# Counting put-off rows four tiles at a time in a graph-network kernel, with their scatters pinned in GpSimd's order

## The chip, the cores and the metric

The kernel runs on one core of a Trainium2 chip. The metric is the device time of one execution in microseconds (us). A NeuronCore has a matrix engine (TensorE, PE in the profile, with its weight loads as PEld), a vector engine (VectorE, DVE), a scalar engine (ScalarE, ACT), GpSimd (POOL) and SyncE (SP), which only issues transfers. Each engine runs its own instructions in their order and waits on semaphores for the others.

## The reference

Four graph layers run one after the other over 4096 nodes with 256 features and one 4096 x 4096 adjacency matrix `adj`; after each, `x = layernorm(x + layer(x))`. Layers 0, 2 and 3 multiply the adjacency with the features and apply a weight matrix. Layer 1 takes two steps of attention in which each row keeps only its largest probabilities, up to a mass of 0.9:

```python
def _top_p_attention(X, W1, W2, W3):
    logits = (X @ W1.T @ W2.T) @ (X @ W3.T).T
    probs = softmax(logits, axis=-1)
    idx = argsort(-probs, axis=-1)
    cs = cumsum(sorted probs)
    mask = cs - sorted probs < 0.9          # put back in the row's order
    A = probs * mask
    return A / max(A.sum(-1, keepdims=True), 1e-12)

R = S + eye; R = R / R.sum(-1, keepdims=True)        # here S is adj
for n in range(2):
    A = _top_p_attention(Xa, W1, W2, W3)
    Xf = R @ Xf
    Xa = A @ Xa
    Z = Z + Xf @ U1[n].T + Xa @ U2[n].T
return layernorm(X + Z) * ln_g + ln_b
```

## The kernel before

The 4096 rows are 32 tiles of 128 rows (`NT = 32`, `P = 128`). The program runs in this order: layer 0, attention step 0, attention step 1, layers 2 and 3 (whose matmuls are L175).

Each attention step is a loop in `run_step` over iterations i = -2 to 31, software-pipelined over three tiles. In iteration i the logits of tile i + 2 are made in eight chunks (L414 on PE, copied by ACT at L415); for tile i + 1, the candidate called `cd`, DVE finds the cut (`peak_groups` with MAX8 at L433, the maximum at L465 and L466, then `tops` with L528 and L532, `pick` to L564); tile i is multiplied (`pieces`). In step 0 a row keeps few entries, so the product of tile i gathers 16 rows of x per row through GpSimd (`gather`, L672) and multiplies by diagonals (L761). In step 1 the row of probabilities is masked by DVE (`settle`: a match-replace over 4096 columns at L658, then the mask in four quarters at L663), transposed by PE (`turn`, L744), copied by ACT (L747) and multiplied (L767). Beside it run the products of R (`neighbours`, L683, L686, ended by L688), one row tile in most iterations, and for the finished tile `mix` (L820, L822) and, in step 1, two layer norms (the power on GpSimd at L199, then L846 and L204). `settle` of tile i + 1 must be done before `pieces` of tile i + 1 begin.

`ops` is a dictionary: `at(g, f)` runs f after piece g (0 to 7) of the iteration. A scheduler then reorders instructions on each engine by its own estimates, within what data and buffers allow, but not across a conditional block (`tc.If`).

**Put-off rows.** Some rows cannot be cut by the quick search. `pick` sets `bad` to 1 for them. `flag` (L582) counts them: PE multiplies `bad` with a matrix of ones (L592, the tile's number of bad rows in every partition) and with a strictly triangular matrix (L593, the bad rows ahead of each one); DVE adds the running base (L595), forms a slot for each row (L599, L600), and GpSimd scatters the row numbers into a list in DRAM (L606). Rows that are not bad go to spare slots. PE, DVE and POOL thus each take part once per tile, in piece 4 of the iteration.

Later the listed rows are worked off in groups of 128 (`put_off`): read the list (L886, L888), gather the rows, make a query and logits, the peak (L471), five probes for the threshold (L498), candidates (L512, L433), tops, pick, a conditional exact search (L648), and `settle` with three match-replaces and the mask. It is a generator: `advance(job)` runs it to its next `yield`, at pieces 1 and 6 of each iteration. `LATER = (1, 3)` gives one group in step 0 and three in step 1; `starts` says after which iteration each begins, and `finish` runs what is left of one before the next and multiplies its rows:

```python
starts = {min((k + 1) * NT // LATER[n] - 1, NT - 2): k for k in range(LATER[n])}
```

That is iteration 30 in step 0, and 9, 20 and 30 in step 1. The groups of step 1 are called the first, second and third here. After iteration 31 the second group's product runs beside 16 tiles of the next layer's `zu` (L869), and the third group's work beside the other 16; then a rest loop (`left_over`) runs zero or more times. `half("mm")` gives the two halves of one PSUM bank (`mm_bank`) in turn, for counting, queries and `mix`.

Of the kernel before, what the change touches and what calls it, by code (L numbers as in the profile page):

```python
# [40 lines left out]
LATER = (1, 3)  # L41
ROUNDS = 9
NG_LATER = 18
KEPT = 16
MATCHES_LATER = 3
MATCHES = 1
# [10 lines left out]
def gnn_stack(ctx, tc, x, adjt, adjn, w0, b0, w1, w2t, w3t, u1t, u2t, ln_g, ln_b, w2, b2, w3, b3, out):  # L57
# [28 lines left out]
    def half(bank):  # L86
        turns[bank] ^= 1
        return (mm_bank if bank == "mm" else acc_bank)[:, turns[bank], :]
# [268 lines left out]
    with tc.tile_pool(name="l1", bufs=1, reuse_waits="tile") as l1:  # L357
# [64 lines left out]
        def small(tag, w=1, dt=F32, bufs=2):  # L422
            if cur["late"]:
                return cur["lw"].tile([P, w], dt, tag=tag, name=f"{tag}_l", bufs=2 if w == 1 else 1)
            return work.tile([P, w], dt, tag=tag, name=tag, bufs=bufs)
# [108 lines left out]
        def pick(st, rounds):  # L534

            top, thr, base = st["top"], st["thr"], st["base"]
            W = 8 * rounds  # L540
            cs = small("cs", W + 1, bufs=1)
            if base is None:
                nc.vector.memset(cs[:, 0:1], 0.0)
                te = small("te", W + 1)
                nc.scalar.activation(te, top, AF.Exp, bias=st["m"], scale=1.0)
            else:
                nc.vector.tensor_copy(cs[:, 0:1], base)
                te = top
            nc.vector.memset(cs[:, W:], 3e38)
            nc.vector.tensor_tensor_scan(cs[:, 1:W], te[:, : W - 1], te[:, : W - 1], cs[:, 0:1], op0=ALU.add, op1=ALU.max)  # L550
            under, part = small("under", W, bufs=1), small("part", W, bufs=1)
            count = small("count")
            nc.vector.tensor_scalar(under, cs[:, :W], thr, 0.0, op0=ALU.is_lt, op1=ALU.add, accum_out=count)
            nc.vector.scalar_tensor_tensor(part, cs[:, 1:], thr, under, op0=ALU.is_ge, op1=ALU.mult)
            st["t"] = t = small("t_thr")
            nc.vector.scalar_tensor_tensor(part, part, 1.0, te[:, :W], op0=ALU.mult, op1=ALU.mult, accum_out=t)
            st["left"] = left = small("left")
            nc.vector.tensor_scalar(part, te[:, :W], t, 0.0, op0=ALU.is_ge, op1=ALU.add, accum_out=left)
            nc.vector.tensor_sub(left, left, count)
            st["bad"] = bad = small("bad")  # L560
            nc.vector.tensor_tensor(bad, te[:, W - 1 : W], te[:, W:], op=ALU.max)
            nc.vector.tensor_tensor(bad, bad, t, op=ALU.is_ge)
            most = 0.0 if sparse(st) else 8.0 * (MATCHES if base is None else MATCHES_LATER)
            nc.vector.scalar_tensor_tensor(bad, left, most, bad, op0=ALU.is_gt, op1=ALU.max)  # L564
            if sparse(st):

                same = small("same")
                for r in range(8, W, 8):
                    nc.vector.tensor_tensor(same, top[:, r - 1 : r], top[:, r : r + 1], op=ALU.is_equal)
                    nc.vector.tensor_tensor(bad, bad, same, op=ALU.max)  # L570
                st["w"] = w = small("w", W)
                kept = small("kept")
                nc.vector.scalar_tensor_tensor(w, te[:, :W], t, te[:, :W], op0=ALU.is_ge, op1=ALU.mult, accum_out=kept)
                whole(st, kept)
# [7 lines left out]
        def flag(st):  # L582


            pb = half("mm")
            later = st.get("later")
            if later is None:
                nc.tensor.matmul(pb[:1, 0:1], st["bad"], ones_col, start=True, stop=True)
                st["nb"] = small("nbad", 1, I32)[:1, :]
                nc.scalar.copy(st["nb"], pb[:1, :1])  # L590
                return
            nc.tensor.matmul(pb[:, 0:1], ones_sq, st["bad"], start=True, stop=True)  # L592
            nc.tensor.matmul(pb[:, 1:2], before, st["bad"], start=True, stop=True)  # L593
            sofar, slot = small("sofar"), small("slot")
            nc.vector.tensor_add(sofar, later["base"], pb[:, 0:1])  # L595

            i = st["tile"]
            at, rows_i = slots_of[cur["n"]][:, i : i + 1], ids[:, i : i + 1]
            nc.vector.scalar_tensor_tensor(slot, pb[:, 1:2], later["base"], spare, op0=ALU.add, op1=ALU.subtract)  # L599
            nc.vector.scalar_tensor_tensor(at, slot, st["bad"], spare, op0=ALU.mult, op1=ALU.add)  # L600
            later["base"] = sofar
            if i == NT - 1 and cur["n"] == 0:

                st["to"] = to = small("to_last", 1, I32, 1)
                nc.vector.scalar_tensor_tensor(to, st["bad"], float(P), rows_i, op0=ALU.mult, op1=ALU.add)
            nc.gpsimd.indirect_dma_start(  # L606
                out=list_d[cur["n"]], out_offset=bass.IndirectOffsetOnAxis(ap=at, axis=0), in_=rows_i, in_offset=None)

        def bit_by_bit(st):

# [331 lines left out]
        def run_step(n, es):  # L942

            later = {"base": spare0}
            tiles = {}
            last = []
            jobs = []
# [26 lines left out]
                cur["late"] = False  # L976
                return [[f] for f in after(n, job["st"])]

            starts = {min((k + 1) * NT // LATER[n] - 1, NT - 2): k for k in range(LATER[n])}
            for i in range(-2, NT):  # L980
                st = tiles.pop(i, None)
                cd = tiles.get(i + 1)
                nxt = None
                if i + 2 < NT:

                    nxt = {"tile": i + 2, "q": cur["qs"].pop(0), "e": logits_in(es[i % 2]), "later": later, "G": {}}
                    tiles[i + 2] = nxt
                if i + 1 == NT and n == 0:
                    for fs in last:
                        for f in fs:  # L990
                            f()
                    last = []
                    left_over(n, es[NT % 2], later)
                ops = {}

                def at(g, f, *args):
                    ops.setdefault(g, []).append(lambda: f(*args))

                for g, fs in zip((1, 2), last):
                    for f in fs:  # L1000
                        at(g, f)
                if 0 < i + 2 < NT - 1:
                    turned = []
                    g = 1 if n else 6
                    at(g - 1, lambda i, turned: turned.append(transposed(cur["xa"][:, i + 3, :])), i, turned)
                    at(g, lambda turned: cur["qs"].append(query(None, turned[0])), turned)
                if cd is not None:
                    peak_groups(cd, NG_LATER if n else ngr)
                    at(1, exp_rows, cd)
                for job in jobs:  # L1010
                    at(1, advance, job)
                if cd is not None:
                    rounds = ROUNDS if n else KEPT // 8
                    at(2, tops, cd, rounds)
                    at(2, pick, cd, rounds)
                    at(4, flag, cd)
                    if n == 0:
                        for k in range(8):
                            at(4 + k // 2, gather, cd, k)
                    else:  # L1020
                        at(5, lambda cd: [None for _ in settle(cd)], cd)
                if n == 0 and st is not None:
                    for k in range(8, KEPT):
                        at(k // 2 - 4, gather, st, k)
                for job in jobs:
                    if n and i + 1 == NT:
                        at(4, advance, job)
                    at(6, advance, job)
                if i + 1 == NT and n == 0:
                    cur["next"] = load_halves(es[1 - NT % 2], xf_d, nc.sync)  # L1030
                if i < 0:
                    now = FIRST[n][i + 2]
                else:
                    now = [i + 2] if FIRST[n][1][-1] < i + 2 < NT else []
                pieces(n, st, nxt, ops, now)
                last = [[f] for f in after(n, st)] if st is not None else []
                if i in starts:
                    k = starts[i]
                    if len(jobs) > (i == NT - 2):
                        last = finish(jobs.pop(0), last)  # L1040
                    e = es[NT % 2] if k + 1 == LATER[n] else es[2]
                    jobs.append({"stages": put_off(n, k, e, later)})
                    if i < NT - 2:
                        advance(jobs[-1])
# [185 lines left out]
```

## Time and profile before

| what | us |
|---|---|
| median of 3 runs | 3214.06 (3208.3 to 3225.59) |
| the profiled execution's own time | 3106.69 |
| its span, from the first to the last instruction | 3105.0 |
| PE busy in it | 2902.2 (93%) |
| DVE busy | 2253.7 (73%) |
| ACT busy | 1725.0 (56%) |
| POOL busy | 779.8 (25%) |
| mean granted PE clock | 0.976 |

The profiled execution is 3.3% shorter than the median of the timed runs. Step 0 lies between about 360 and 1280 us of the span, step 1 from there to about 2550, layers 2 and 3 to the end. A line of the group view reads: source line, engine, operation, output and inputs by the program's names, shape, count, then times. An entry of the waits reads: who waited, for whom, total us, times, longest us. A line of the timeline reads: start, duration, engine, source line, operation, names, shape, number of merged instructions, and in brackets the idle time before it and what ended it. A row of the stretches reads: from and to, length, then busy time and number of instructions of PE, PEld, DVE, ACT and POOL, then the PE clock, the DMA share and GB/s.

### The profile page before, as it was taken

What the parts mean: (1) busy time and instruction counts of PE and PEld (TensorE: products, weight loads), DVE (VectorE), ACT (ScalarE), POOL (GpSimd) and SP (SyncE); (2) the same over time, 40 slices, a digit from 0 to 9 for tenths busy, and PEclk for the clock granted to TensorE, in tenths of its full rate; (3) what the DMA queues carried; (4) which work ended last, traced back from release to release, by engine and by line L of the source; (5) the groups of instructions that cost most, each with busy time, mean ns of one, the idle gap of its engine ahead of it and who ended that gap; (6) DMA issues with size and microseconds to landing.
All of it is one profiled execution on the core that took longest, in us unless ns stands there. A gap on an engine that the chain in (4) does not pass through costs nothing. (4 is left out here: it accounts for less than half of the span.)

```text
span 3105.0 us, 45412 instructions
## 1 busy us (share of the span) xinstructions
PE 2902.2 (93%) x14244; PEld 2300.0 (74%) x14244; DVE 2253.7 (73%) x7159; ACT 1725.0 (56%) x2883; POOL 779.8 (25%) x908
## 2 busy tenths in 40 slices
PE   7999889999999997799999999999999978999998
PEld 3788677788878875577777877878878546777886
DVE  4666688888888884379997999959998725443444
ACT  2555566666666655364555555546554426666664
POOL 1111167777777772000000000010001110000000
PEclk9999999999999998899999999999999998999999
DMA  9996378888878873310000111101111324333332
GB/s 170 158 176 136 66 131 138 164 153 154 147 153 155 161 149 112 117 50 25 25 21 25 37 34 38 30 31 35 39 35 32 115 88 152 107 107 97 107 107 78
DMA packets 247484, 299.44 MB, mean 96 GB/s; under 512 B 34464, under 2 KB 201312, under 8 KB 247232
## 3 DMA queue, kind: packets, MB, share of 16 engines
q0 software_dynamic: 46336, 104.28, 23.8%
q1 hardware_dynamic: 188656, 180.93, 18.9%
q10 hardware_dynamic: 12240, 11.23, 1.1%
q8 instruction: 115, 1.88, 0.3%
q14 instruction: 137, 1.12, 0.2%
HBM read 330.65 MB, written 66.32 MB: 128 GB/s over the span
## 5 line engine op out<-in xcount | busy, mean ns | idle before, releaser
L686 PE MATMUL acc_r<-xh,adjq 128*128 128x512 f32 x2048 | 617.1, 430 | 20.9 <-ACT adjq L683 12.0
L767 PE MATMUL acc_bank<-xa,at 128*128 128x256 f32 x2240 | 548.1, 385 | 25.8 <-ACT at L747 25.4
L672 POOL DMA_INDIRECT G<-x_d,cols x512 | 496.6, 970 | 214.4 <-PE acc_bank L761 77.6
L683 ACT CAST adjq<-adj 128x512 fp32r<-128x512 fp8e4 x512 | 316.2, 620 | 399.5 <-PE acc_r L686 318.8
L767 PEld LDWEIGHTS acc_bank<-xa,at 128*128 128x128 f32 x2240 | 408.4, 192 | 84.3 <-ACT at L747 37.1
L686 PEld LDWEIGHTS acc_r<-xh,adjq 128*128 128x128 f32 x2048 | 378.9, 191 | 110.4 <-ACT adjq L683 31.8
L433 DVE MAX8 cand<-e 128x8 f32<-128x228 f32 (+1 forms) x1088 | 386.6, 399 | 71.1 <-ACT e L415 69.5
L199 POOL TENSOR_TENSOR rstd<-ve,mhalf 128x1 f32<-128x1 f32 x166 | 100.3, 604 | 1330.9 <-DVE ve L197 1287.5
L415 ACT COPY e<-lg 128x512 f32<-128x512 f32 x544 | 315.0, 585 | 183.7 <-PE lg L414 179.9
L414 PE MATMUL lg<-kS,q 128*128 128x512 f32 x1088 | 385.0, 439 | 0.1
L1110 ACT CAST a<-a 128x1024 fp32r<-128x1024 fp8e4 x256 | 268.1, 1049 | 167.9 <-PE acc L175 127.9
L761 PE MATMUL acc_bank<-G,dg 128*128 128x256 f32 x1024 | 272.2, 387 | 12.5 <-DMA adj<-adj_d 5.4
L530 DVE FIND_INDEX8 cols<-top,e 128x8 uint32<-128x4096 f32 x64 | 282.8, 4419 | 0.0
L175 PE MATMUL acc<-xh,a 128*128 128x512 f32 x1024 | 261.9, 410 | 21.0 <-DMA x2i<-x_d 17.1
L175 PE MATMUL acc<-y0h,a 128*128 128x512 f32 x1024 | 250.0, 398 | 0.0
L175 PEld LDWEIGHTS acc<-xh,a 128*128 128x128 f32 x1024 | 193.5, 192 | 67.7 <-ACT xh L151 22.2
L175 PE MATMUL acc<-yh,a 128*128 128x512 f32 x1024 | 237.9, 394 | 0.0
L761 PEld LDWEIGHTS acc_bank<-G,dg 128*128 128x128 f32 x1024 | 196.6, 193 | 49.5 <-DVE dg L759 10.0
L175 PEld LDWEIGHTS acc<-yh,a 128*128 128x128 f32 x1024 | 192.3, 188 | 43.6
L175 PEld LDWEIGHTS acc<-y0h,a 128*128 128x128 f32 x1024 | 188.1, 188 | 38.8 <-issue 0.6
L747 ACT COPY at<-at_ps 128x512 f32<-128x512 f32 x288 | 168.8, 588 | 83.0 <-PE at_ps L744 81.3
L414 PEld LDWEIGHTS lg<-kS,q 128*128 128x128 f32 x1088 | 180.1, 192 | 20.4 <-ACT e L415 6.4
(287 smaller groups left out, 4430.3 us busy)
## 6 DMA issues: line engine op xcount, KB each, us to landing
adj<-adj_d SPq DMA_DIRECT2D x256, 128.0 KB
a<-adj_d SPq DMA_DIRECT2D x256, 128.0 KB
a<-in_adjt POOLq DMA_DIRECT2D x64, 256.0 KB
adj_d<-a SPq DMA_DIRECT2D x64, 256.0 KB
adjn<-in_adjn POOLq DMA_DIRECT2D x64, 256.0 KB
x_d<-x SPq DMA_DIRECT2D x64, 128.0 KB
xf_d<-xf_new SPq DMA_DIRECT2D x64, 128.0 KB
xf<-xf_d SPq DMA_DIRECT2D x64, 128.0 KB
```

The lines of the kernel that those rows point to most:

```text
L175: nc.tensor.matmul(acc, a[:, j, :], halves(jt), start=(jt == 0), stop=(jt == NT - 1))
L414: nc.tensor.matmul(pl[:, :LC], q[k], kS[:, s], start=(k == 0), stop=(k == 1))
L415: nc.scalar.copy(l[:, s], pl[:, :LC])
L433: nc.vector.max(dst[:, 8 * g : 8 * g + 8], src[:, g * w : min((g + 1) * w, N)])
L530: nc.vector.max_index(st["at"][:, 8 * r : 8 * r + 8], t8, st["e"][:, :N])
L672: nc.gpsimd.indirect_dma_start(out=g, out_offset=None, in_=x1_d, in_offset=bass.IndirectOffsetOnAxis(ap=st["at"][:, k : k + 1], axis=0))
L683: nc.scalar.copy(a, cur["a8"][:, g % 2 * GP : (g % 2 + 1) * GP, :])
L686: nc.tensor.matmul(acc_r, a[:, j, :], xf[:, jt, :], start=(jt == 0), stop=False)
L747: nc.scalar.copy(at[:, :G, :], ps[:, :G, :])
L761: nc.tensor.matmul(acc_a, dg[:, k % 4, :], st["G"][k], start=(k == 0), stop=(k == KEPT - 1))
L767: nc.tensor.matmul(acc_a, ats[g][:, j, :], cur["xa"][:, jt, :], start=(jt == 0), stop=(jt == NT - 1))
L1110: nc.scalar.copy(a, a8)
```

## The change

`flag` no longer counts each tile. `pick` writes `bad` into a column of a four-column tile `bads`; when the fourth column is full (tiles 3, 7, 11, ...), or for each of the last four tiles alone, one pair of matmuls counts all columns, a scan adds the running base, and four more DVE operations form the slots. The scatters are put on a list `pend` and issued singly: one from each `flag`, and one more at a fixed place in each iteration (piece 0 in step 0, piece 3 in step 1), and all that are left ahead of a group's start. Each is pinned behind the instructions traced before it on GpSimd. In step 1 `flag` moves from piece 4 to piece 7, and the counting matmul is pinned behind what PE was given before it. `starts` is rounded up to the next iteration i with i % 4 == 3: iterations 11, 23 and 30 in step 1 instead of 9, 20 and 30; in step 0 it stays 30.

```diff
+AT_ONCE = 4
...
-            st["bad"] = bad = small("bad")
+            later = st.get("later")
+            if later is None:
+                st["bad"] = bad = small("bad")
+            else:
+                if later["from"] is None:
+                    later["from"] = st["tile"]
+                    later["bads"] = work.tile([P, AT_ONCE], F32, tag="bads", name="bads", bufs=2)
+                c = st["tile"] - later["from"]
+                st["bad"] = bad = later["bads"][:, c : c + 1]
...
-            nc.tensor.matmul(pb[:, 0:1], ones_sq, st["bad"], start=True, stop=True)
-            nc.tensor.matmul(pb[:, 1:2], before, st["bad"], start=True, stop=True)
-            sofar, slot = small("sofar"), small("slot")
-            nc.vector.tensor_add(sofar, later["base"], pb[:, 0:1])
-
-            i = st["tile"]
-            at, rows_i = slots_of[cur["n"]][:, i : i + 1], ids[:, i : i + 1]
-            nc.vector.scalar_tensor_tensor(slot, pb[:, 1:2], later["base"], spare, op0=ALU.add, op1=ALU.subtract)
-            nc.vector.scalar_tensor_tensor(at, slot, st["bad"], spare, op0=ALU.mult, op1=ALU.add)
-            later["base"] = sofar
...
-            nc.gpsimd.indirect_dma_start(
-                out=list_d[cur["n"]], out_offset=bass.IndirectOffsetOnAxis(ap=at, axis=0), in_=rows_i, in_offset=None)
+            if i % AT_ONCE == AT_ONCE - 1 or i >= NT - AT_ONCE:
+                first, bads = later["from"], later["bads"]
+                w = i + 1 - first
+                later["from"] = None
+                pb = half("mm")
+                total = nc.tensor.matmul(pb[:, :w], ones_sq, bads[:, :w], start=True, stop=True)
+                if n:
+                    tc.keep_in_program_order(total)
+                nc.tensor.matmul(pb[:, AT_ONCE : AT_ONCE + w], before, bads[:, :w], start=True, stop=True)
+                sofar, slot = small("sofar", AT_ONCE + 1), small("slot", AT_ONCE)
+                nc.vector.tensor_copy(sofar[:, 0:1], later["base"])
+                nc.vector.tensor_tensor_scan(sofar[:, 1 : w + 1], pb[:, :w], bads[:, :w], sofar[:, 0:1], op0=ALU.add,
+                                             op1=ALU.max)
+                nc.vector.scalar_tensor_tensor(slot[:, :w], pb[:, AT_ONCE : AT_ONCE + w], spare, sofar[:, :w],
+                                               op0=ALU.subtract, op1=ALU.add)
+                nc.vector.tensor_mul(slot[:, :w], slot[:, :w], bads[:, :w])
+                nc.vector.tensor_scalar(slots_of[n][:, first : i + 1], slot[:, :w], spare, None, op0=ALU.add)
+                later["base"] = sofar[:, w : w + 1]
+                later["pend"] += range(first, i + 1)
+            scatter(later)
+
+        def scatter(later, most=1):
+
+            for k in later["pend"][:most]:
+                tc.keep_in_program_order(nc.gpsimd.indirect_dma_start(
+                    out=list_d[cur["n"]], out_offset=bass.IndirectOffsetOnAxis(ap=slots_of[cur["n"]][:, k : k + 1], axis=0),
+                    in_=ids[:, k : k + 1], in_offset=None))
+            later["pend"] = later["pend"][most:]
...
-            starts = {min((k + 1) * NT // LATER[n] - 1, NT - 2): k for k in range(LATER[n])}
+            starts = {}
+            for k in range(LATER[n]):
+                i = (k + 1) * NT // LATER[n] - 1
+                starts[min(i + (AT_ONCE - 1 - i) % AT_ONCE, NT - 2)] = k
...
+                if i < NT - 2:
+                    at(3 if n else 0, scatter, later)
...
-                    at(4, flag, cd)
+                    at(NLC - 1 if n else 4, flag, cd)
...
                 if i in starts:
+                    scatter(later, NT)
```

More of the change, by code (lines that the diff above doesn't have):

```diff
@@ L582, in flag @@
         def flag(st):
-            pb = half("mm")
             later = st.get("later")
             if later is None:
+                pb = half("mm")
                 nc.tensor.matmul(pb[:1, 0:1], st["bad"], ones_col, start=True, stop=True)
@@ L600, in flag @@
-            nc.vector.scalar_tensor_tensor(at, slot, st["bad"], spare, op0=ALU.mult, op1=ALU.add)
-            later["base"] = sofar
-            if i == NT - 1 and cur["n"] == 0:
-                st["to"] = to = small("to_last", 1, I32, 1)
-                nc.vector.scalar_tensor_tensor(to, st["bad"], float(P), rows_i, op0=ALU.mult, op1=ALU.add)
-            nc.gpsimd.indirect_dma_start(
-                out=list_d[cur["n"]], out_offset=bass.IndirectOffsetOnAxis(ap=at, axis=0), in_=rows_i, in_offset=None)
+            i, n = st["tile"], cur["n"]
@@ new lines, in flag @@
+            if i == NT - 1 and n == 0:
+                st["to"] = to = small("to_last", 1, I32, 1)
+                nc.vector.scalar_tensor_tensor(to, st["bad"], float(P), ids[:, i : i + 1], op0=ALU.mult, op1=ALU.add)
+            if i % AT_ONCE == AT_ONCE - 1 or i >= NT - AT_ONCE:
+                first, bads = later["from"], later["bads"]
+                w = i + 1 - first
+                later["from"] = None
+                pb = half("mm")
+                total = nc.tensor.matmul(pb[:, :w], ones_sq, bads[:, :w], start=True, stop=True)
[12 more added lines that the diff above has]
+                later["pend"] += range(first, i + 1)
@@ L942, in run_step @@
         def run_step(n, es):
-            later = {"base": spare0}
+            later = {"base": spare0, "from": None, "bads": None, "pend": []}
             tiles = {}
```

## The prediction, made before the changed kernel had run

> **What bounds the kernel now.** I read the tenths by slice first, then busy time by stretch, then the idle time before the counting matmuls (L592), then the order of time around them. The slices show TensorE (PE) full nearly throughout, and VectorE (DVE) full beside it only in the second attention step (slices 18 to 30):
>
> ```profile
> PE   7999889999999997799999999999999978999998
> DVE  4666688888888884379997999959998725443444
> ```
>
> Busy time in three stretches (us; PE, weight loads, DVE, ACT, POOL): the steady part of step 0, step 1 with the R products up to the maximum of tile 25, and from there to the first masked quarter of tile 31:
>
> ```profile
> 500.00:1150.00 650.00, 649.58 (x3685) 519.91 (x3684) 569.74 (x1692) 421.49 (x822) 477.61 (x506) 1.00 0.84 153
> ...
> 1656.00:2171.00 515.00, 490.07 (x2470) 405.95 (x2470) 450.78 (x1518) 285.35 (x480) 38.82 (x49) 0.98 0.12 33
> 2171.00:2393.00 222.00, 210.93 (x1073) 175.01 (x1073) 210.94 (x730) 117.79 (x194) 15.63 (x20) 1.00 0.15 32
> ```
>
> Step 0 is PE alone, without gaps, 24.43 us a tile. In the second stretch PE leads (490 of 515; gaps 26.5, of which 9.2 before L592), DVE has 59 us of gaps. In the third both stand at 95%: DVE is as full as PE.
>
> What one tile's counting costs PE in step 0, by the timeline (start, us):
>
> ```profile
> 720.31 0.40 PE L696 MATMUL nef_ps<-adjn,adj 128*128 128x128 fp8e4 x4
> 720.54 0.34 PE L592 MATMUL mm_bank<-bad,ones_sq 128*128 128x1 f32 x2
> 720.74 0.36 PE L593 MATMUL mm_bank<-bad,before 128*128 128x1 f32 x2
> 720.96 0.71 PE L414 MATMUL lg<-kS,q 128*128 128x512 f32 x2
> ```
>
> From 720.54 to 720.96, so 0.42 us, nothing else enters PE. In step 1 PE also waits there, because `bad` is not ready (us in total, times, longest; 1640 to 2400):
>
> ```profile
> PE mm_bank L592 <- DVE bad L564: 15.8, 15, 1.7
> ```
>
> Last, the end of step 1 on DVE: tile 31's maximum, its match-replace, its mask, its slots, and the list read back:
>
> ```profile
> 2375.41 0.30 DVE L465 TENSOR_REDUCE m<-cand 128x1 f32<-128x144 f32 x1
> ...
> 2386.81 4.43 DVE L658 MATCH_REPLACE8 e<-match,e 128x4120 f32<-128x4120 f32 x1
> 2391.41 1.28 DVE L663 SCALAR_TENSOR_TENSOR e<-e,t_thr 128x1024 f32<-128x1024 f32 x1
> 2393.46 0.21 DVE L600 SCALAR_TENSOR_TENSOR slots<-slot,bad,spare 128x1 int32<-128x1 f32 x1
> ...
> 2403.88 0.15 DVE L888 TENSOR_SCALAR from_l<-to_l 128x1 int32<-128x1 int32 x1 [6.01 <-DMA to_l<-list_d]
> ```
>
> PE cannot begin tile 31's transposes before L663, and the last put-off group cannot begin before the list. From there PE runs full to the end of the step (zu tiles, 84.6 us busy in 2420 to 2511), so what delays this point delays the end.
>
> **What the Trainium skill says.** "TensorE: Matmul & The Clock Gate", The mechanism: matmuls keep strict program order, so one that waits holds those behind it; the 15.8 us before L592 agree. "VectorE: DVE Perf Modes", Rules for kernel authors: minimize the number of operations, since each pays its own fixed part; agreed, as L595, L599 and L600 take 155, 211 and 204 ns for one column. "Perfetto Trace Analysis", Optimization Strategy: where a kernel has several regimes, interleaving them can help. The trace agrees that it does here: the second put-off group ends (L658 and L663 between 2275 and 2302) beside R products, and PE idled only 3.2 us between 2270 and 2320.
>
> **The change, part by part.**
>
> *Fewer countings, step 0.* 32 pairs become 11 (seven groups of four, then the last four tiles singly): 21 × 0.42 = 8.8 us less on PE, which is the bound. A pair of four columns isn't in the trace; it adds three columns to each matmul, and 1024 columns of L414 took 0.54 us (720.96 to 721.50), so under 0.01 us. **−8.8.** DVE's three operations give way to five a group; hidden, as DVE is at 88% here. GpSimd (POOL) issues the same 32 scatters, but two in some iterations and none in others. Its gathers (L672) start 1.25 us apart (711.75, 713.00), so 16 of them, two adjn loads and one scatter fill about 23.5 of the 24.4 us. A second scatter (1.16 us, L606) puts it about 1 us behind, and the next tile without one gives that back, with 12 gather buffers between: 0, at most +4 over the step if gathers come late.
>
> *First nine tiles of step 1* (period 29.3 us, a ring: last logits chunk, DVE's tops and match-replace, query, logits). The pair costs PE 0.36 here (1466.87 to 1467.23) and lies on the ring: 9 × 0.36 = 3.2 less. The two groups' pairs are pinned to the end of the iteration, where PE waits for ACT anyway (1.36 us at 1450). Their five DVE operations fall among the tops, on the ring: by the built program's order between L465 and the third L528. A scan over four columns isn't in the trace: above the 155 ns of a one-column operation, below the 229 ns of the scan over 15; I take 0.2, and 0.6 us a group after overlap: +1.2. The scatters move from between the tile's two `rstd` (L199) to outside the pair; the 1.15 us that L204 waits goes, but DVE then waits for ACT's last logits instead. **−2.0.**
>
> *Stretch to 2171.* 14 pairs become 4: −4.2. The stalls of 9.2 before L592 go. The put-off groups also start later (`starts` 9 and 20 become 11 and 23), so the peak (4.42) and three probes of the second one leave this stretch: 4.42 + 3 × 6.22 (two probes follow each other at 2428.52 and 2434.74) = 23 us of DVE. As PE leads here that buys little: I take 4 of the other 17 us of PE gaps. **−17.5** (from −4, if the stalls only move to L744, to −33, if DVE's whole relief counts).
>
> *From tile 25's maximum to tile 31's mask.* Those 23 us come here, plus 4 single countings at 0.4: 24.5 us more on an engine with 9 us of gaps in 222. Concretely, the built order puts the second group's `If` (L648), its three match-replaces and its mask (3 × 4.43 + 4 × 1.28 + about 1 = 19.4 us) behind tile 31's max8 and ahead of its tops. All of tile 31's L528, L658, L663 queue behind them, and PE, with R(31) done and no logits left, waits. **+24.5** (12 to 30).
>
> *Last list.* Tile 31's flag moves from piece 4 to piece 7, and in DVE's order its slots come behind all four L663 instead of the first: 3 × 1.21 = **+3.6** on scatter, list read and gather; PE already waits 1.27 us for that gather (2408.54). The added wait is PE's, with pieces of tile 31 and the group's logits behind it.
>
> *Moved starts otherwise, order of POOL, the extra branch place:* the list reads of the first two groups (DVE idle 5.2 and 5.7 us) may come a little earlier; PE leads there, 0.
>
> Sum: −8.8 − 2.0 − 17.5 + 24.5 + 3.6 = **−0.2 us** on the profiled execution's 3106.7 (span 3105.0), that is 3106.5. The median of the runs is 3214.06, 3.5% above that execution; I carry the difference over: **3214**.
>
> **The rivals.**
>
> *A, no change* (0.34): the sum. About 28 us are taken away on PE and 28 are given back at the end of step 1.
>
> *B, faster* (0.34): the late work of the second group hides better than I think, since the freed stretch can reach DVE's own limit. With −33 in place of −17.5 and the rest as above: −15.7; with tile 31's delay at 12 instead of 24.5 as well: −28. That is 3198 to 3186. For it: DVE's 59 us of gaps up to 2171. Against it: half of them are waits for ACT's logits, so for PE.
>
> *C, slower* (0.24): the stalls before L592 only move. PE in program order then meets the same late DVE one instruction later, at the transposes (L744) which need the mask. Where both engines stand at 95%, a PE that is released early gains nothing. Then the stretch gives 4.2 − 4 more lost = 0, and −8.8 − 2.0 + 0 + 27 + 3.6 = +20: 3234. It decides from the point where the stretch gives under 4 us. For it: L592 stalls only in tiles where a put-off group loads DVE. Against it: at 2129.97 PE reached L744 with no wait right after a tile with a stall.
>
> *D, the change does not do what it says in step 1* (0.08): the scheduler's order there moves neither stalls nor the group's end, and only step 0 counts: −8.8, so 3205, inside no change.
>
> **How the numbers follow.** Half a per cent, 16 us, is about what a measurement of this kernel can tell from no change; the three runs before spread over 17 us. B's middle lies beyond it on one side, C's on the other. No change's own range is 3198 to 3230. To hold 8 in 10 I reach into B and C by their bounds, with 6 us for the spread of runs: 3182 to 3242. Faster 0.34 (B), same 0.42 (A and D), slower 0.24 (C).
>
> **What would show it.** Step 0: the tile period falls from 24.43 to about 24.0 in tiles without a count. L592's line shows 22 pairs instead of 64 (x44 for x128 instructions) and no wait for `bad`. Tile 25's maximum comes earlier by about 28 us in all; then 19 us of the group's L658 and L663 stand between tile 31's L465 and its L658, and PE has a gap of about 20 us before the L744 of tile 31. If that gap is absent I am wrong in the direction of B; if L744 in the middle of step 1 shows waits of about 1 us per tile for the mask, in the direction of C. If step 0's period doesn't fall, PE was not the bound there.

## The result: slower, by 2.3% in one kind of session and by 4.0% in another

The changed kernel took 3289.96 us (median of 4 runs), the kernel before beside it 3216.65: ratio 1.0234, interval 1.0214 to 1.0255. The forecast was 3214, so no change.

One thing has to be known first. The sessions in which the kernels ran are of two kinds for this program. In those of one kind, here X, the median of the kernel before is 3208 to 3217 us; in those of the other, Y, 3106 to 3120. The recorded expectations call the two kinds chips, but a session of each kind carries the same chip number, 2, so what makes the difference is open. The profile of before that the prediction read (own time 3106.69) fits Y, the times beside it are of X. Both kernels therefore have a second profile, taken on Y: before 3115.9 us of span (`before2`), after 3244.5 (`after2`); there the changed kernel took 3245.46 (median of 2) against 3119.82, ratio 1.0403 (1.0377 to 1.0429). Every comparison of profiles below is between runs of Y unless X is named, and every ratio is to the kernel before in the same session.

The tenths by slice of POOL in the kernel before, then of PE and POOL in the changed kernel:

```profile
POOL 1111167777777772000000000010001110000000
...
PE   7999897899889886879999799997998796999998
...
POOL 1121266566556655000000000001000100000000
```

PE is no longer at 9 throughout step 0 (slices 6 to 16), and POOL went down there from 7 to 5 and 6. Busy time in the steady part of step 0 (PE, weight loads, DVE, ACT, POOL) says the same:

```profile
500.00:1150.00 650.00, 577.89 (x3134) 457.41 (x3134) 493.17 (x1440) 366.74 (x713) 415.99 (x445) 0.95 0.79 135
```

PE had 649.58 of these 650 us before; now no engine is full. What they wait for there, longest sums first and others left out (us, times, longest; 450 to 1245):

```profile
POOL list_d L630 <- DMA list_d<-ids,slots: 93.7, 15, 9.6
...
PE nef_ps L722 <- DMA adjn<-in_adjn: 71.0, 16, 10.3
...
PE acc_bank L787 <- DMA G<-x_d,cols: 24.9, 12, 8.1
```

The first line is the cause, as experiments 2, 5 and 6 show: GpSimd stood 93.7 us before a list scatter (L630), waiting for the transfer of an earlier list scatter. The other two follow from it: PE waits for the gathers that GpSimd issues, and for its loads of `adjn`, the adjacency tiles of the product in L722. In the kernel before, PE's wait for `adjn` was 7.7 us in all (experiment 5). One group of four on POOL, by the timeline (start, us, then the wait ahead of it):

```profile
812.82 1.45 POOL L698 DMA_INDIRECT G<-x_d,cols  x1 [0.30 <-PE acc_r L712]
814.57 1.00 POOL L630 DMA_INDIRECT list_d<-ids,slots  x1 [0.30 <-issue]
815.88 0.96 POOL L698 DMA_INDIRECT G<-x_d,cols  x1 [0.30 <-issue]
817.14 0.95 POOL L698 DMA_INDIRECT G<-x_d,cols  x1 [0.30 <-PE acc_bank L787]
824.90 1.00 POOL L630 DMA_INDIRECT list_d<-ids,slots  x1 [6.80 <-DMA list_d<-ids,slots]
...
828.42 0.61 POOL L718 DMA_DIRECT2D adjn<-in_adjn  x1
```

The second scatter comes two gathers after the first, writes the same tensor, and starts only 10.3 us after it. Everything behind it on POOL, the gathers and the adjn load, is late by 6.8 us; the third scatter at 835.38 loses another 6.34. In the kernel before the scatters of step 0 stood more than 22 us apart, so this wait could not show.

By stretches between tile maxima (L465 before, L466 after), span of before and after on Y, us:

| stretch | before | after | difference | forecast |
|---|---|---|---|---|
| step 0, tile 0 to tile 31 | 772.2 | 864.4 | +92.2 | -8.8 |
| to tile 0 of step 1 | 169.2 | 173.7 | +4.5 | 0 |
| step 1, tile 0 to 9 | 279.5 | 276.0 | -3.5 | -2.0 |
| tile 9 to 25 | 582.2 | 558.6 | -23.6 | -17.5 |
| tile 25 to the first masked quarter of tile 31 | 221.0 | 276.6 | +55.6 | +24.5 |
| from there to the end | 712.6 | 715.3 | +2.7 | +3.6 |

(The nine-tile forecast started at tile 0, the next one at tile 11; between 9 and 11 nothing was forecast but the counting. The two profiles of the kernel before differ by 7.8 us in step 0 and by 3.2 us from tile 9 to 25, so a difference of that size between two single profiles says little there.)

### The profile page after: what moved, and what is told of

Read it like the earlier page. It is cut to its first block, busy times and chain, and to the rows that moved or that the text cites. A ratio compares the mean times of both kernels' runs of the same rounds, so it can differ in the third digit from the quotient of the medians.

```text
span 3296.3 us, 44974 instructions
## 1 busy us (share of the span) xinstructions
PE 2929.2 (89%) x14076; PEld 2308.8 (70%) x14076; DVE 2255.1 (68%) x7077; ACT 1724.5 (52%) x2883; POOL 773.8 (23%) x908
## 5 line engine op out<-in xcount | busy, mean ns | idle before, releaser
L712 PE MATMUL acc_r<-xh,adjq 128*128 128x512 f32 x2048 | 632.5, 436 | 25.6 <-ACT adjq L709 15.7
L793 PE MATMUL acc_bank<-xa,at 128*128 128x256 f32 x2240 | 543.4, 384 | 36.6 <-ACT at L773 36.2
L698 POOL DMA_INDIRECT G<-x_d,cols x512 | 500.7, 978 | 279.5 <-PE acc_bank L787 113.0
L793 PEld LDWEIGHTS acc_bank<-xa,at 128*128 128x128 f32 x2240 | 409.2, 192 | 96.8 <-ACT at L773 48.3
L712 PEld LDWEIGHTS acc_r<-xh,adjq 128*128 128x128 f32 x2048 | 386.4, 194 | 117.2 <-ACT adjq L709 32.2
L415 PE MATMUL lg<-kS,q 128*128 128x512 f32 x1088 | 392.1, 444 | 8.0 <-issue 6.8
L787 PE MATMUL acc_bank<-G,dg 128*128 128x256 f32 x1024 | 283.6, 399 | 35.2 <-DMA G<-x_d,cols 14.8
```

The lines of the kernel that those rows point to most:

```text
L415: nc.tensor.matmul(pl[:, :LC], q[k], kS[:, s], start=(k == 0), stop=(k == 1))
L698: nc.gpsimd.indirect_dma_start(out=g, out_offset=None, in_=x1_d, in_offset=bass.IndirectOffsetOnAxis(ap=st["at"][:, k : k + 1], axis=0))
L712: nc.tensor.matmul(acc_r, a[:, j, :], xf[:, jt, :], start=(jt == 0), stop=False)
L787: nc.tensor.matmul(acc_a, dg[:, k % 4, :], st["G"][k], start=(k == 0), stop=(k == KEPT - 1))
L793: nc.tensor.matmul(acc_a, ats[g][:, j, :], cur["xa"][:, jt, :], start=(jt == 0), stop=(jt == NT - 1))
```

## Experiments

The sessions on X held experiments 1 to 3, those on Y the rest.

**1. Fewer scatters an iteration (X).** `spread0`:

```
-                if i < NT - 2:
+                if i < NT - 2 and (n or i > 25):
                     at(3 if n else 0, scatter, later)
```

> The changed kernel, but in step 0 at most one scatter goes out in an iteration (tiles 0 to 27), as in the kernel before; counting by fours and all of step 1 stay. Theory 1 (a scatter into the list waits in GpSimd's order until the one before it has landed, 8 to 10 us, and the gathers queue behind it): no scatter of step 0 waits for the list any more (about 80 us in the changed kernel's profile), and the time falls from 3290 to about 3215 to 3235. Theory 2 (counting by fours or the pinned order upsets step 0, whatever the distance of the scatters): stays within 10 us of 3290. Theory 3 (the loss lies in step 1: moved group starts, later slots): stays within 10 us of 3290, with step 0 as long as before.

Measured: 1.0184 (1.0158 to 1.0210), 3270. The edit did not do what I had meant: the first scatter of a group, late in its iteration, and the second, early in the next, were still 10 us apart, and 38 us of waits for the list were left of 85. Step 0 went from 920.1 to 889.7 us. It falls between the theories and settles nothing by itself, but the dose goes with the effect.

**2. Four lists in turn in step 0 (X).** The scatters stay as close, but consecutive ones write different tensors. `fourlists0`:

```
-    out=list_d[cur["n"]]
+    out=lists[cur["n"]][0 if cur["n"] else k % 4]
...
+    for k in range(4):
+        nc.sync.dma_start(four[:, k : k + 1], lists[n][k][slots, :])
+    nc.vector.tensor_reduce(to, four, axis=AX.X, op=ALU.min)
```

> The changed kernel with its scatters two an iteration, but in step 0 into four lists in turn (tile number modulo 4), which are read back together and merged by a minimum; so consecutive scatters write different tensors and need not wait for each other. Theory 1: the waits for the list go although the scatters stand as close as before, time 3215 to 3240 (three more list reads at the end of step 0 cost up to 5). Theory 2 (the place of two scatters among the gathers, not the wait): 3280 to 3300. Theory 3: 3280 to 3300.

Measured: 1.0142 (1.0115 to 1.0169), step 0 867.6 us in place of 920.1. The scatters on POOL, by the timeline:

```profile
706.97 1.01 POOL L631 DMA_INDIRECT list_d<-ids,slots  x1 [0.30 <-issue]
708.28 1.00 POOL L631 DMA_INDIRECT alt_d<-ids,slots  x1 [0.30 <-issue]
715.27 1.02 POOL L631 DMA_INDIRECT alt_d<-ids,slots  x1 [0.30 <-issue]
```

The second now goes out 1.3 us after the first, without a wait. So the wait is for the tensor, and without it step 0 is 52 us shorter, though the two scatters now stand even closer. Theory 1 had expected at most 3240; at 3254 the run is still 46 us over the kernel before, so something else remains.

**3. One step undone at a time (X).** `old0` counts every tile of step 0 by itself (`if n == 0 or i % AT_ONCE == ...`), `old1` every tile of step 1, with starts 9, 20, 30, the flag in piece 4 and no pinned count.

> The changed kernel with every tile of step 0 counted by itself and scattered at once, one an iteration; step 1 as changed. Theory 1: step 0 as in the kernel before, 3215 to 3240; what remains above 3216 is step 1's. Theory 3: about 3290.

> The changed kernel with step 1 counted tile by tile as in the kernel before (starts 9, 20, 30, flag in piece 4, one scatter an iteration, no pinned counting); step 0 as changed. Theory 1: still slow, 3270 to 3295. Theory 3: 3205 to 3220.

Measured: `old0` 1.0153 (1.0127 to 1.0178), step 0 867.0 us, the same as with four lists; `old1` 1.0206 (1.0179 to 1.0233). Both steps lose, step 0 more. The two remainders, 50 and 69 us, add up to more than the whole change (73 to 82 us on X). Either a third part is common to both, or the two do not simply add.

**4. The kernel before again, and the form without grouping (Y).** `before2` is the kernel before, unchanged. `once1` has `AT_ONCE = 1`, flag in piece 4, no pinned count: one scatter an iteration, but five DVE operations a count and pinned scatters.

> The kernel before, unchanged, profiled again: its first profiled execution (3107) lies 100 us under the median of its timed ones (3208 to 3216), while the profiled executions of the changed kernel and its variants agree with their medians. Theory A: the first profile caught an execution whose step 0 ran without short pauses of all engines, and the usual one has them: this profile spans 3200 to 3220, with tile periods of 26 to 30 us in step 0 in place of 24.4 and step 1 as in the first profile (m of tile 0 to m of tile 31: 1063 us). Theory B: the extra 100 us lies elsewhere (step 1 or the last layers).

> The changed kernel with groups of one: each tile counted by itself and scattered in its iteration, starts 9, 20, 30, flag in piece 4; what remains of the change is the pinned order of the scatters and five VectorE operations per count in place of three. Undoing the change in one step alone left +50 (step 0 undone) and +69 (step 1 undone) over the kernel before, 119 together against 82 for the whole change: so some 37 us may come from what both still had. Theory P (pins and extra operations cost by themselves): 3235 to 3255. Theory 1 alone: within 10 us of the kernel before, 3200 to 3220.

Measured: `before2` 3119.11 (ratio 1.0002), the session's before 3118.92; its profile has a step 0 at 24.43 us a tile like the first one. So the 100 us lie between sessions, and not between a profiled execution and the others, as both theories had assumed. They lie mostly in step 0: counted tile by tile in both, it takes 867.0 us in `old0` on X and 789.2 in `once1` on Y. `once1` 1.0070 (1.0052 to 1.0088), 22 us, of which 17.0 in step 0. That is a part common to both steps' variants, though less than the sums of experiment 3 ask for.

**5. Four lists in both steps (Y).** `fourboth`; and with the edit of `spread0` on top, `fourspread`.

> The changed kernel with four lists in turn in both steps (step 0 alone gave 3254 against 3290). In step 1 the changed kernel's profile has the list read of the first two groups late (31 us of waits for it on VectorE, against 5), behind scatters that went out one after the other. Theory 1 (waits of scatter for scatter): 15 to 30 us under the step-0 version, 3225 to 3240. Rival (those waits lie beside other work): same as the step-0 version, 3246 to 3258.

> The changed kernel with four lists in turn in both steps, and in step 0 at most one scatter in an iteration (tiles 0 to 27). With four lists but two scatters an iteration step 0 was still 33 us longer than in the kernel before, on the chip where that takes 3119. Theory F (the second scatter in an iteration overfills GpSimd and the gathers behind come late): step 0 within 20 us of the kernel before, 10 to 25 us less than with two an iteration: ratio 1.010 to 1.015 where that had 1.018. Rival (counting by fours itself, or the pin): step 0 as long as with two, ratio 1.018 again.

Measured: `fourboth` 1.0183 (1.0163 to 1.0203) against 1.0403 for the changed kernel on Y. Step 0: 804.8 in place of 864.4, 60 us less, and the 93.7 us of scatters waiting for the list are gone. Step 1, tile 9 to 25: 546.9 in place of 558.6. There the scatters of a group's last tiles had queued ahead of the list read, by POOL's timeline of the changed kernel:

```profile
1804.19 1.02 POOL L630 DMA_INDIRECT list_d<-ids,slots  x1 [0.17 <-issue]
1811.58 0.95 POOL L630 DMA_INDIRECT list_d<-ids,slots  x1 [6.37 <-DMA list_d<-ids,slots]
1819.95 0.96 POOL L630 DMA_INDIRECT list_d<-ids,slots  x1 [7.42 <-DMA list_d<-ids,slots]
```

and DVE then stood until the list had come (waits, 1755 to 2494, us, times, longest; second line PE):

```profile
DVE from_l L914 <- DMA to_l<-list_d: 32.1, 2, 17.3
...
PE tr L186 <- DMA xf_new<-xa_d,from_l: 18.1, 1, 18.1
```

Before, the two waits for the list were 6.4 and 5.2. Four lists do not bring that back: the four reads go out one after another, and in `fourboth` DVE still waits 25.7 us for them.

`fourspread` 1.0130 (1.0113 to 1.0148), step 0 793.0: the second scatter in an iteration costs 12 us more even where it waits for no other. 21 us of step 0 over the kernel before remain. PE shows where, by its waits in step 0, first in the kernel before (450 to 1152), then in `fourspread` (450 to 1175):

```profile
PE nef_ps L696 <- DMA adjn<-in_adjn: 7.7, 3, 5.9
...
PE nef_ps L723 <- DMA adjn<-in_adjn: 35.0, 17, 6.8
```

With 4.7 us for gathers it is 32 us more in all. So here too PE waits for transfers that GpSimd issues late; the counting itself is not what is slow.

**6. Distance alone (Y).** The kernel before, counting untouched, its scatters of step 0 held back and sent two an iteration: eight gathers apart in `pairs0`, four in `close0`.

```
+            later["held"].append(i)
+            if i % 4 == 3 or i >= NT - 4:
+                later["pend"] += later["held"]
+                later["held"] = []
+            scatter(later)          # close0: scatter(later, 2)
...
+                    at(0, scatter, later)   # pairs0 alone
```

> The kernel before with one edit in step 0: the scatters of four tiles are held back and go out two an iteration, eight gathers (some 11 us) apart in GpSimd's order; counting stays tile by tile. Theory 1 (what costs is that a scatter waits for the one before to land, 8 to 10 us): hardly any wait for the list, at most 15 us over the kernel before. Theory F (two scatters in an iteration overfill GpSimd, whose 16 gathers, two loads and one scatter already take 23.5 of 24.4 us): 25 to 60 us over.

> As the run with pairs eight gathers apart, but both scatters of an iteration go out four gathers (some 5 us) apart, two iterations with two and two with none. Same number of scatters per iteration, only closer. Theory 1: one wait of 3 to 5 us in each iteration with two, 14 of them, GpSimd late by that, 25 to 60 us over the kernel before. Theory F: the same as with eight gathers between.

Measured: `pairs0` 1.0095 (1.0071 to 1.0119), 26 us; `close0` 1.0233 (1.0209 to 1.0257), 72 us. Two scatters of `pairs0`, then two of `close0`, on POOL:

```profile
773.10 1.01 POOL L618 DMA_INDIRECT list_d<-ids,slots  x1 [0.30 <-issue]
786.70 1.01 POOL L618 DMA_INDIRECT list_d<-ids,slots  x1 [0.30 <-issue]
```

```profile
821.19 1.38 POOL L618 DMA_INDIRECT list_d<-ids,slots  x1 [0.30 <-issue]
834.61 0.99 POOL L618 DMA_INDIRECT list_d<-ids,slots  x1 [7.01 <-DMA list_d<-ids,slots]
```

In `close0` every second scatter stood 4 to 10 us; the fourteen between 430 and 1165 add up to 85 us. The trace puts only 3 of them down to the list, the others to an instruction that was done earlier or to none; that they too waited for it is read from the distance to the first, 10 to 14 us in all. Step 0 is 78.3 us longer than in the kernel before. The same scatters a little further apart cost 20.6. So both theories hold a part, and the distance is the larger one.

**7. Step 1 alone (Y).** `step1`: step 0 as before, step 1 as changed.

> Step 0 as in the kernel before (counted and scattered tile by tile, no pin), step 1 as changed (one list, starts 11, 23, 30). By the two profiles of one chip step 1 and the tail account for some 32 us of 126: moved late work ahead of tile 31 20 us, the rest list reads behind scatters and the first group's product. Theory: 28 to 40 us over the kernel before, step 0 as before. Rival (step 1's loss is a sequel of the disturbed step 0): within 10 us of the kernel before.

Measured: 1.0113 (1.0096 to 1.0131), 38 us; step 0 771.5, as before. Step 1's loss stands by itself.

**8. An earlier second group (Y).** `starts19`: starts 11, 19, 30 in place of 11, 23, 30.

> The changed kernel with the second put-off group of step 1 started in iteration 19 in place of 23. Theory 1b (the second group's match-replaces and mask ahead of tile 31's tops open the gap of 23 us on TensorE at the end of step 1): those stand before tile 28, the gap goes, 15 to 25 us less than the changed kernel: 3265 to 3275. Rival (the work displaces other work of the same length): 3285 to 3295.

Measured: 1.1097 (1.1076 to 1.1118), 342 us over the kernel before; a miss. The gap did go: from tile 31's maximum to its first masked quarter 14.8 us in place of 36.6. But the third group got twelve tiles, and a fifth list read shows that its 128 rows did not do and the left-over loop ran. The fifth list read on DVE:

```profile
2659.09 0.15 DVE L914 TENSOR_SCALAR from_l<-to_l 128x1 int32<-128x1 int32 x1
```

From the mask to the end it is 964.9 us in place of 715.3: one pass of the loop costs 250.

**9. The price of a counting pair (Y).** `double0`: the kernel before, the pair of step 0 issued twice.

> The kernel before, with the pair of counting matmuls of step 0 issued twice for every tile (the second pair's sums are used by nothing). The prediction priced a pair at 0.42 us of a TensorE that is the bound in step 0. Right: 13 us over the kernel before (32 x 0.42), and step 0's tile period 24.43 becomes 24.85. Rival (the pair fits between GpSimd's gathers, which set the period): within 4 us.

Measured: 1.0037 (1.0026 to 1.0049), 12.5 us, and tile periods of 24.88. On PE:

```profile
725.09 0.33 PE L592 MATMUL mm_bank<-bad,ones_sq 128*128 128x1 f32 x2
...
725.51 0.36 PE L595 MATMUL mm_bank<-bad,ones_sq 128*128 128x1 f32 x2
725.73 0.36 PE L596 MATMUL mm_bank<-bad,before 128*128 128x1 f32 x2
725.96 0.71 PE L414 MATMUL lg<-kS,q 128*128 128x512 f32 x2
```

The second pair takes 725.51 to 725.96, 0.45 us. The prediction's price was right, and PE was the bound.

**10. Two more DVE operations (Y).** `dve2`: a copy and a maximum added to each count of step 0.

> The kernel before with two more one-column VectorE operations after each tile's count in step 0 (a copy and a maximum with itself, on the way to the next tile's base), five in place of three as in the changed kernel; GpSimd's order is unchanged. The changed kernel with groups of one took 22 us over the kernel before, 17 of them in step 0, where it differs by these two operations and by a scatter that stands after four gathers in place of three (the pin moves nothing there). Theory V (VectorE's operations): 10 to 20 us over the kernel before. Theory G (the place of the scatter among the gathers): within 4 us.

Measured: 1.0003 (0.9993 to 1.0013). Theory V falls. (The two operations stand behind the slots here and ahead of them in `once1`, but there no scatter of step 0 after 450 us waited more than 0.3 us.) The traces leave the scatter's place, after four gathers in `once1` and after three in the kernel before. That is by exclusion only: no run moved the scatter alone or took the pin away, and the scan and the shared tile `bads` of `once1` are not in `dve2`. The 17 us of `once1` are no cost of each tile: after the first six, most tile periods are 24.4 us as before, and three are 27.7 to 29.5.

**11. Both kernels' better halves (Y).** `best`: step 0 as before; step 1 by fours, into four lists, starts 10, 22, 30.

> Step 0 as in the kernel before (each tile counted and scattered by itself, no pin); step 1 as changed, but with four lists in turn and the put-off groups started at 10, 22 and 30 in place of 11, 23 and 30. Theory: step 1's first tiles keep their 0.45 us a tile, the list reads no longer stand behind scatters, and half of the gap of TensorE at the end of step 1 goes: 5 to 20 us under the kernel before. If the second group's late work still stands ahead of tile 31's tops: 0 to 20 us over.

Measured: 3113.93 against 3119.82, ratio 0.9982 (0.9973 to 0.9992): faster than both, but than the kernel before by 0.2% only. From tile 31's maximum to its mask it is 15.9 us, as before: the second group's match-replaces now stand ahead of that maximum. They are not free there: the stretch from tile 25 to that mask is 10.5 us longer than in the kernel before, the one from 9 to 25 12.9 shorter.

**12. The changed kernel again (Y).** `after2`, unchanged.

> The changed kernel, unchanged, on whatever chip this is. The kernel before took 3208 to 3217 on one chip and 3119 on another (its first profile, 3107, is of the second kind), so profiles of the two kernels must come from one chip. If this chip is of the 3119 kind: step 0 (maximum of tile 0 to maximum of tile 31) some 95 us longer than the 764 to 772 of the kernel before, as in the run with the second group started at 19, step 1 some 30 us longer, in all 3235 to 3260. If it is of the 3208 kind: 3280 to 3300 again.

This was the run of the changed kernel on Y, used throughout: 1.0403, inside what was expected.

## Why the prediction was wrong

**Counting in step 0, -8.8.** The price was right (experiment 9). Most of it could not be collected, because PE stopped being the bound. Where GpSimd was not behind, the saving did show: after the first groups, of each four tile periods one is 24.0 us, as forecast, one 24.4, and the other two are 28 to 35. No run counts by fours in step 0 with the scatters left at their old places.

**"0, at most +4 over the step", the order of POOL.** This step failed: +92.2. I priced a second scatter by its time on POOL, 1.16 us, and asked whether the gathers would come late by that. The wait was put at nothing: in this program a scatter does not start before the last one into the same tensor has landed, 9.5 to 11.0 us after that one's start. The size could be guessed from the lines I had shown: slots at 2393.46, list back at 2403.88, so 10.4 us for a scatter and the read behind it. And the built order, which I had read, has two gathers between the first scatters of a group. Taking away 85 to 94 us of such waits in step 0 gave 52 us on X and 60 on Y (experiments 2 and 5); the second scatter in an iteration without a wait costs 12 (experiment 5). The last 21 us have the gain of counting in them, so the cost behind is larger by up to 8.8. It shows as late adjn loads; why GpSimd issues these late where no scatter waits for another is not settled beyond experiment 10. By my own estimate GpSimd was busy 23.5 of 24.4 us a tile, so little of a wait could be caught up: that should have been the warning.

**First nine tiles, -2.0.** -3.5: right in sign and near in size; its parts were not measured apart.

**The stalls before the count.** They went as forecast, but half came back. PE's waits for `bad` were 15.8 us in 1640 to 2400. The waits of the changed kernel up to tile 31's maximum (1755 to 2494; the count of tile 31 comes after it, see below):

```profile
PE acc_bank L793 <- ACT at L773: 24.8, 7, 16.6
...
PE at_ps L770 <- DVE e L689: 7.8, 6, 1.6
...
PE mm_bank L611 <- DVE bads L573: 0.7, 2, 0.6
```

Before the counts (L611) 0.7 us are left. At the transposes (L770), where the kernel before has no such wait, there are 7.8 now, 1.3 us each in six tiles. That is the mechanism of rival C at half its size. (C's sum also has 27 for the 24.5 of the next part, without a reason.) The rest of the loss has other causes.

**Tile 25 to tile 31's mask, +24.5; the stretch ahead, -17.5.** For the end of the step the mechanism was right to the line. The end of step 1 on DVE, tile 31's maximum, then the second group's (`match_l`, `t_thr_l`), then its own:

```profile
2492.65 0.30 DVE L466 TENSOR_REDUCE m<-cand 128x1 f32<-128x144 f32 x1
...
2503.26 4.43 DVE L684 MATCH_REPLACE8 e<-match_l,e 128x4120 f32<-128x4120 f32 x1
...
2524.76 4.43 DVE L684 MATCH_REPLACE8 e<-match,e 128x4120 f32<-128x4120 f32 x1
...
2529.24 1.27 DVE L689 SCALAR_TENSOR_TENSOR e<-e,t_thr 128x1024 f32<-128x1024 f32 x1
...
2534.06 0.20 DVE L622 TENSOR_SCALAR slots<-slot,spare 128x1 int32<-128x1 f32 x1
...
2545.44 0.15 DVE L914 TENSOR_SCALAR from_l<-to_l 128x1 int32<-128x1 int32 x1 [10.72 <-DMA to_l<-list_d]
```

and PE beside it:

```profile
2523.24 0.58 PE L611 MATMUL mm_bank<-bads,ones_sq 128*128 128x1 f32 x2 [16.31 <-DVE bads L573]
...
2530.67 1.94 PE L770 MATMUL at_ps<-ident,e 128*128 128x128 f32 x8 [6.41 <-DVE e L689]
```

16.31 + 6.41 = 22.7 us of idle PE, where I had said about 20. Two terms were missing. The first group's product goes where the second group starts (`finish(jobs.pop(0), last)`): the long period of about 66 us was tile 22 to 23 and is now tile 25 to 26, so some 30 us left one stretch and entered the other. Without it the stretch ahead is 6 longer in place of 17.5 shorter, the last one 26 longer as forecast. (The 59 us of DVE gaps in the stretch ahead, on which rival B leaned, are 64 by the row that was shown, 515 less 450.78.) And the list reads, which "may come a little earlier" and were put at 0, came later, behind scatters that waited for each other, and PE paid for it. At the first group it stood 18.1 us for the group's rows (L186, experiment 5). At the second, DVE waited for the list and so held back tile 25's maximum, ACT's exponential behind it and the copy that PE needed: the 16.6 us of L793 above. At the two places in the kernel before, PE stood 7.3 and 4.0 us. That is 23 us more, about what the stretch misses against its forecast (24 us); 12 of them a run shows (experiment 5), the rest is matched by size alone.

**Last list, +3.6.** +2.7; right in size.

**The median, by carrying a difference over.** The 3.5% between the profiled execution and the runs lay between two kinds of session, not between profile and runs. The ratio is smaller on X. Its step 0 is the slower one (experiment 4), so the scatters may have had more room there; no profile of the kernel before on X shows it.

## To carry to other kernels

Before moving transfers in a queue, look which of them write the same tensor, and price the distance between them with the time to land, not the time to issue; where they are closer than that, the queue can stop, and all behind it with it. Rotating a few destination tensors took the wait of scatter for scatter away here, at the price of a read for each of them. When late work starts later, list everything its start carries along, and look at which last consumer it will stand in front of.

## What was not expected of the hardware

From one list scatter of 128 numbers to the next one that waited for it, it took 9.5 to 11.0 us in step 0 of the changed kernel (first to second and second to third of its groups, after 600 us), with the DMA engines busy 79% of the time, and still 7.4 and 8.4 us in step 1 (1804.19 to 1811.58 to 1819.95) with them at 5% (1800 to 1820): most of it is there without the load.

The same program takes 3% longer on X than on Y. In each profile of X engines stand 29 to 46 times, 67 to 123 us summed over them, for a releaser that the trace gives only as remote, all in step 0 or just behind it; in those of Y never. What it is stays open.
